# Two metaformer layers on one core: where dt's softplus is made, who copies the carried columns, and how far ahead scans are served

## The chip, the cores and the metric

The kernel runs on one core of a Trainium2 chip, as one program with one launch. The metric is the device time of an execution in microseconds. Before the change it is 5492.92 us, the median of three runs (5492.4 to 5493.44). An execution recorded by the hardware profiler took 5501.81 us; the span of its instructions is 5500.0 us. All times below come from that profiled execution unless the three runs are named.

A core has TensorE (PE in the profile), VectorE (DVE), ScalarE (ACT), GpSimd (POOL) and SyncE (SP, which only issues DMAs here). Each takes its instructions from a queue of its own, in order; semaphores tie the queues together.

## The reference

Input x is (4, 384, 32, 32) in float32. Layer 0 adds a selective scan over four directions of the image (rows and columns, forward and backward) and then a feed-forward network whose weights are Kronecker products. Layer 1 adds a Mamba block, with two halves of 384 inner channels, and then a mixture of four experts of which each token uses two. The part that the change touches is the selective scan, which both layers have:

```
dt = softplus(dts @ W_dt + bias)                  # softplus(v) = ln(1 + exp(v))
step(h, t):                                       # for each channel d and state n
    h  = exp(dt[d,t] * A[d,n]) * h + dt[d,t] * u[d,t] * B[n,t]
    y[d,t] = sum over n of h[d,n] * C[n,t]
```

There are 16 states, 384 channels in a pass, and 1024 positions in a sequence. The recurrence runs over t, so the second half of a sequence starts from the h that the first half left.

## The kernel before

**Passes and steps.** Sequences are cut into halves of T = 512 columns. A pass is one half of one direction (layer 0) or one half of one group of 384 channels (layer 1). There are 32 + 16 = 48 passes; the order of the passes mixes the layers and batches (L1362). A pass has three chunks of 128 channels and four groups of four states, so 12 steps, 576 in all. A step works on four tiles x = 0..3, each with 32 channels times 4 states on the 128 partitions and 512 columns along the free dimension. Every second pass is marked "first": it starts from zero and leaves its last column to the other half (the column at T - 1, or at 0 for a direction that runs backwards).

**A step.** ScalarE makes four decays exp(dt A) into the four PSUM tiles `da` (`decay`, L1483 to L1487). GpSimd makes s = dtu * B for all four at once, 128 x 2048 (`times_b`, L1481). VectorE runs the recurrence with one scan instruction for each x (`scan`, L1489 to L1501). The first scans of a step write into `da` in PSUM, and VectorE then multiplies them with C into s (`times_c`, L1526); the others write into s in place, and GpSimd multiplies those with C (`times_c_pool`, L1535). TensorE sums over the states into the PSUM tile `acc` (`add`, L1512 to L1517), and after four steps VectorE adds `acc` to the result (`gather`; L593, L597, L599, L819). There are four s tiles, so the product with B of step i waits for the sum of step i - 4.

**How many of a step's four products VectorE takes** is decided by `split` (L1620): if GpSimd is far ahead of the time at which its next product with B is needed (by more than SPARE), VectorE takes two; if it is less than C1 ahead, all four; else three. `share` holds the answer.

**The carried columns.** In a first pass, VectorE copies the last column of each scanned tile to the tile `state`, two copies behind each pair of scans (`keep_state`, L1503 to L1510). In the other half the scan takes its start from there.

**dt.** `prep_pass` (L464 to L501) makes dt for a whole pass: three matmuls (L476), for each of them an addition of the bias from PSUM into the SBUF tile `dt` (L485), then |v|, exp(-|v|) and ln(1 + .) over all 1536 columns in SBUF (L490), and dt = max(v, 0) + that on VectorE (L492). GpSimd multiplies with u (L497). Both tiles go to DRAM and are read back, spread over the partitions, part by part (`spread_out`, `spread_pass`; the loads of `dts` are issued on ScalarE's queue).

**The order of the instructions** is fixed when the program is built. A planner (`Plan.run`) keeps a clock for every engine and an estimated cost for each operation, and always emits what can start first. The scans and what they need are main streams: `decays` on ScalarE, `cs` and `bs` on GpSimd, `gathers` and `main` on VectorE, `adds` on TensorE. Everything else (layer norms, feed-forward network, projections, routing, experts, `prep_pass`) runs as side lanes that name, with `yield`, the engine and the cost of what comes next. `choose` (L1632) lets a side operation of ScalarE or GpSimd go ahead of a main one if it ends before that one is due. The due time comes from `needed` (L1585), which takes the next instruction of VectorE's stream and adds STEP for each step and an offset AT within the step. An `Op` has a cost and, for `adds`, a lag: the planner lets it begin that much later than its inputs' end. Three PSUM tiles `ps` serve all side work, taken and given back one at a time.

Of the kernel before, what the change touches and what calls it, by code (L numbers as in the profile page):

```python
# [12 lines left out]
AF = mybir.ActivationFunctionType  # L13
ALU = mybir.AluOpType
# [11 lines left out]
T = 512  # L26
# [224 lines left out]
def layers(ctx, tc, ins, out, const):  # L251
# [212 lines left out]
    def prep_pass(v, p, of_u):  # L464


        q, h = v["q"], v["h"]
        spread = dram.tile([2, NC, QP, NG, T], F32, tag="dts", name="dts", bufs=3)
        dt, dtu = yield from tmp.two(True)
        if v["layer"]:  # L470
            yield SP, LOAD
            nc.sync.dma_start(out=dtw[dt_rows(q), :], in_=ins["w_dt1"][:, v["c0"] * P : (v["c0"] + NC) * P])
        for c in range(NC):
            pd = yield from ps.take(True)
            yield PE, 1.2
            nc.tensor.matmul(  # L476
                pd,
                lhsT=dtw[dt_rows(q), c * P : (c + 1) * P],
                rhs=xd[dt_rows(q), cols(h)],
                start=True,  # L480
                stop=True,
            )
            bias = pv(v["dtb"], v["c0"] + c, 1)
            yield ACT, 0.7
            nc.scalar.activation(dt[:, c, :], pd, AF.Identity, bias=bias)  # L485
            ps.give(pd)

        for func, of, more in ((AF.Abs, dt, {}), (AF.Exp, dtu, {"scale": -1.0}), (AF.Ln, dtu, {"bias": 1.0})):
            yield ACT, 1.45
            nc.scalar.activation(dtu, of, func, **more)  # L490
        yield DVE, 3.15
        nc.vector.scalar_tensor_tensor(dt, dt, 0.0, dtu, ALU.max, ALU.add)  # L492
        spread_out(spread[0], dt)
        for c in range(NC):
            yield POOL, 1.3 if len(of_u(dt[:, c, :], c)) == 1 else 1.75
            for (to, u), (by, _) in zip(of_u(dtu[:, c, :], c), of_u(dt[:, c, :], c)):
                nc.gpsimd.tensor_tensor(to, by, u[:, c], ALU.mult)  # L497
        tmp.give(dt)
        yield SP, LOAD
        spread_out(spread[1], dtu)  # L500
        tmp.give(dtu)  # L501
        st["spread", p] = spread
# [986 lines left out]
    def scan(i, x):  # L1489
        p, j = steps[i]  # L1490
        v = passes[p]
        way = slice(None, None, -1) if v["rev"] else slice(None)
        s = ss[i % NSR][:, x, way]
        d = das[x][:, way]
        in_psum = x < share[i] if x else True
        nc.vector.tensor_tensor_scan(  # L1496
            d if in_psum else s, d, s, 0.0 if v["first"] else state[:, v["slot"], j, x : x + 1], ALU.mult, ALU.add
        )
        if not in_psum:
            plan.skip.add(("mult", i, x))  # L1500
            plan.end["da free", i, x] = plan.free[DVE]  # L1501

    def keep_state(i, of):  # L1503

        p, j = steps[i]
        v = passes[p]
        at = 0 if v["rev"] else T - 1
        for x in (2 * of, 2 * of + 1):
            src = das[x] if x < share[i] else ss[i % NSR][:, x, :]
            nc.vector.tensor_copy(state[:, v["slot"], j, x : x + 1], src[:, at : at + 1])  # L1510

    def add(i):  # L1512

# [21 lines left out]
    def times_c_pool(i):  # L1535
        m = share[i]
        s = ss[i % NSR]
        nc.gpsimd.tensor_tensor(s[:, m:, :], s[:, m:, :], rep(cts[i % 4], NG - m), ALU.mult)  # L1538
        for x in range(m, NG):
            plan.end["part", i, x] = plan.end["c", i]  # L1540

    STEP, C1, SPARE = 7.1, 1.29, 2.5
    C = (0.0, 3.5, 2.42, C1, 0.0)
    share = dict.fromkeys(range(N), 3)
    main, gathers, decays, bs, cs, bl, cl, adds = ([] for _ in range(8))

    AT = {"scan": (0.0, 1.27, 3.9, 5.17), "mult": (2.54, 3.22, 6.44, STEP), "state": (2.54, 6.44)}
    for i in range(N):
        p, part, m = place(i)
        v = passes[p]  # L1550
        first = v["first"]
        after = ("state", i, 1) if first else ("scan", i, NG - 1)
        ring = [("add", i - NSR)] if i >= NSR else []
        rows = ("quad", v["q"]["n"])
        if part == 0:
            of_b = [rows] + ([("b", i - 4)] if p else [])
            of_c = [rows] + ([("part", i - 4, x) for x in range(NG)] if p else [])
            bl.append(Op(("bt", p, m), LOAD, of_b, lambda p=p, m=m: load(p, m, NS, bts)))
            cl.append(Op(("ct", p, m), LOAD, of_c, lambda p=p, m=m: load(p, m, 0, cts)))
        bs.append(Op(("b", i), 4.58, [("dtu", p, part), ("bt", p, m), *ring], lambda i=i: times_b(i)))  # L1560
        for x in range(NG):
            free = [("da free", i - 1, x)] if i else []
            decays.append(Op(("da", i, x), 0.69, [("dt", p, part, x // 2), *free], lambda i=i, x=x: decay(i, x)))
        for what, x in (
            ("scan", 0), ("scan", 1), ("state", 0), ("mult", 0), ("mult", 1),
            ("scan", 2), ("scan", 3), ("state", 1), ("mult", 2), ("mult", 3),
        ):
            if what == "scan":
                op = Op((what, i, x), 1.22 if first else 1.28, [("da", i, x), ("b", i)], lambda i=i, x=x: scan(i, x))
            elif what == "state":  # L1570
                if not first:
                    continue
                op = Op((what, i, x), 0.16, [], lambda i=i, x=x: keep_state(i, x))
            else:
                op = Op((what, i, x), 0.69, [("ct", p, m)], lambda i=i, x=x: times_c(i, x))
            main.append(op)
        cs.append(Op(("c", i), C1, [("ct", p, m), after, ("split", i)], lambda i=i: times_c_pool(i)))
        wait = [("gather", (i // 4 - 1) // NC, (i // 4 - 1) % NC)] if m == 0 and i else []
        adds.append(Op(("add", i), 1.0, [("part", i, x) for x in range(NG)] + wait, lambda i=i: add(i), 1.5))
        if m == 3:  # L1580
            cost = 1.35 if v["layer"] == 0 and v["k"] % 2 else 0.75
            room = [] if v["layer"] else [("have", "y", v["b"])]
            gathers.append(Op(("gather", p, part), cost, [("add", i), *room], lambda p=p, c=part: gather(p, c)))

    def needed(plan, i, x):  # L1585

        op = plan.head(DVE, 1)
        if op is None:
            return plan.free[DVE]
        what, j, k = op.key  # L1590
        return max(plan.free[DVE], plan.now) + (i - j) * STEP + x - AT[what][k]

    def due_b(plan):

# [37 lines left out]
    def choose(plan, e, mains, side):  # L1632
        if e == POOL:
            return pool_choice(plan, mains, side)
        if e == DVE:
            for n, (t, k, op) in enumerate(mains):
                if op.key[0] == "scan" and op.key[2] == 1:
                    i = op.key[1]
                    share[i] = split(plan, i, t + 3.6)
                    plan.streams[POOL][0][i].cost = C[share[i]]  # L1640
        best = min(mains, key=lambda x: (x[0], x[1])) if mains else None
        main_of = (best[0], (best[1], best[2])) if best else None
        side_of = (side[0], side[3]) if side else None
        if side is None or main_of is None and e in (SP, PE, DVE):
            return main_of if side is None else side_of
        start, want = side[0], side[3].want
        aged = plan.now - (side[3].ready() + LAG) > age(side[3], e)
        if e == ACT:
            head = plan.head(ACT, 0)
            if head is None:  # L1650
                return side_of
            due = needed(plan, head.key[1], AT["scan"][head.key[2]]) - head.cost - LAG
            if best and best[0] <= start and not aged:
                return main_of
            if start + want[1] <= due or aged:
                return side_of
            return main_of
        if e == PE:
            d, a = plan.head(DVE, 1), plan.head(PE, 0)
            behind = (d.key[1] if d else N) - (a.key[1] if a else N)  # L1660
            if behind > 1 and best[0] <= start:
                return main_of
            return side_of if start <= best[0] + (0.3 if side[3].rank < LOW else -0.3) else main_of
        if e == DVE:
            return side_of if start <= best[0] + 0.1 else main_of
        return side_of if start <= best[0] else main_of
# [5 lines left out]


SWITCH = 2.6
LOAD = 3.0
AGE = {PE: 8.0, ACT: 6.0, POOL: 8.0, DVE: 0.0, SP: 0.0}

# [97 lines left out]
```

## Time and profile before

| | |
|---|---|
| median of three runs | 5492.92 us |
| profiled execution | 5501.81 us |
| its span | 5500.0 us |
| first scan begins, last scan ends | 92 us, 4763 us |
| L1496, the scans on VectorE (2304) | 2771.8 us, 1.21 to 1.27 us each |
| L1487, the decays on ScalarE (2304) | 1520.2 us, 684 ns each |
| L1516, the sums over states on TensorE | 1021.4 us |
| mean granted clock of TensorE | 0.802 |

The busy time of an engine is the sum over its instructions; an engine that waits isn't busy. In the rows by instruction the columns are the line, the engine, the operation, what is written and read, the shape, the count, then the busy time with the mean duration of one in ns, and last how long the engine was idle just before these instructions and what ended that idle time. TensorE's float32 matmuls show two records for each matmul of the program. The row of 40 digits has one digit for each fortieth of the span, the busy share in tenths.

### The profile page before, as it was taken

How to read it: one execution, taken by the hardware profiler on the slowest of the kernel's cores; microseconds unless marked ns; L12 is line 12 of the kernel's file. 1: busy time of each engine (PE TensorE's matmuls, PEld its weight loads, DVE VectorE, ACT ScalarE, POOL GpSimd, SP SyncE). 2: the span in 40 equal slices, each digit the busy share in tenths (PEclk: the TensorE clock that was granted, in tenths of full speed). 3: DMA queues.
4: the chain of work that ended last, by engine and by line, in shares of the span. 5: the costliest groups of instructions: out<-in, count | busy, mean ns of one | idle time of the engine just before them, and what ended most of it. 6: DMA issues, size and time to landing. Idle time of an engine off the chain costs nothing. (4 is left out here: it accounts for less than half of the span.)

```text
span 5500.0 us, 48538 instructions
## 1 busy us (share of the span) xinstructions
PE 4028.5 (73%) x13780; PEld 1779.3 (32%) x13780; DVE 4249.6 (77%) x5670; ACT 3089.9 (56%) x4683; POOL 4280.5 (78%) x1533
## 2 busy tenths in 40 slices
PE   4444467763654788787777878887888876898998
PEld 1000012210121333333334422334323322566775
DVE  4999999988888999888887889898988889510000
ACT  3444457664444577675554667775776654444342
POOL 4999999899898999898887989998988899500101
PEclk7555578775766888898887888898888877899997
DMA  3335464443343554446565554555545444456554
GB/s 112 130 136 198 161 206 157 145 133 128 129 131 122 193 162 142 162 160 195 200 218 169 179 159 140 189 169 192 177 159 177 156 155 162 153 167 198 173 172 154
DMA packets 429094, 896.32 MB, mean 163 GB/s; under 512 B 74612, under 2 KB 176152, under 8 KB 410392
## 3 DMA queue, kind: packets, MB, share of 16 engines
q1 hardware_dynamic: 371608, 701.82, 39.9%
q10 hardware_dynamic: 49024, 166.22, 8.9%
q0 software_dynamic: 8192, 25.17, 1.4%
q8 instruction: 109, 1.79, 0.1%
q14 instruction: 161, 1.32, 0.1%
HBM read 718.11 MB, written 174.95 MB: 162 GB/s over the span
## 5 line engine op out<-in xcount | busy, mean ns | idle before, releaser
L1481 POOL TENSOR_TENSOR s<-dtus,bt 128x2048 f32<-128x2048 f32 x576 | 2620.0, 4553 | 202.9 <-PE acc L1516 101.9
L1487 ACT ACTIVATE da<-dts,a 128x512 f32<-128x512 f32 x2304 | 1520.2, 684 | 1185.4 <-DVE s L1527 835.7
L1516 PE MATMUL acc<-s,four 128*32 128x512 f32 x4608 | 1021.4, 754 | 726.4 <-POOL s L1538 521.3
L1538 POOL TENSOR_TENSOR s<-s,ct 128x1024 f32<-128x1024 f32 (+1 forms) x535 | 1254.8, 2346 | 151.4 <-DVE s L1496 69.8
L1496 DVE TENSOR_TENSOR_SCAN da<-da,s 128x512 f32<-128x512 f32 x617 | 725.3, 1218 | 103.6 <-ACT da L1487 53.8
L1527 DVE TENSOR_TENSOR s<-da,ct 128x512 f32<-128x512 f32 x1242 | 796.5, 680 | 0.2
L1496 DVE TENSOR_TENSOR_SCAN da<-da,state,s 128x512 f32<-128x512 f32 x625 | 770.0, 1272 | 29.2 <-ACT da L1487 17.0
L1496 DVE TENSOR_TENSOR_SCAN s<-da,state,s 128x512 f32<-128x512 f32 x527 | 649.9, 1269 | 42.6 <-ACT da L1487 42.6
L1496 DVE TENSOR_TENSOR_SCAN s<-da,s 128x512 f32<-128x512 f32 x535 | 626.7, 1207 | 14.8 <-ACT da L1487 14.5
L1516 PEld LDWEIGHTS acc<-s,four 128*32 128x32 f32 x4608 | 145.1, 119 | 1406.5 <-POOL s L1538 754.4
L1211 PE MATMUL ps<-tmp,mw 128*128 128x256 f32 (+1 forms) x1884 | 411.7, 375 | 22.3 <-ACT tmp L1183 6.6
L1231 PE MATMUL ps<-mw,tmp 128*128 128x384 f32 x1048 | 402.0, 533 | 21.4 <-ACT tmp L1277 8.5
L1211 PEld LDWEIGHTS ps<-tmp,mw 128*128 128x128 f32 x1884 | 336.9, 203 | 143.7 <-issue 30.5
L708 PE MATMUL ps<-big,w 128*128 128x512 f32 x576 | 302.2, 671 | 83.8 <-DMA w<-in_w_in_dram 80.1
L1322 POOL DMA_INDIRECT tmp<-ys,slot x42 | 40.5, 964 | 349.5 <-DMA ys<-bt 323.2
L497 POOL TENSOR_TENSOR tmp<-tmp,big 128x256 f32<-128x256 f32 (+1 forms) x192 | 198.4, 1058 | 115.5 <-DVE tmp L492 113.6
L1231 PEld LDWEIGHTS ps<-mw,tmp 128*128 128x128 f32 x1048 | 208.8, 207 | 242.0 <-issue 86.6
L476 PE MATMUL ps<-xd,dtw 12*128 12x512 f32 (+1 forms) x288 | 205.6, 817 | 90.0 <-DMA dtw<-in_w_dt_dram 65.1
L492 DVE SCALAR_TENSOR_TENSOR tmp<-tmp,tmp 128x1536 f32<-128x1536 f32 x48 | 262.8, 5475 | 6.5 <-ACT tmp L490 6.2
L1345 DVE TENSOR_TENSOR tmp<-tmp,da 128x384 f32<-128x384 f32 x5 | 2.8, 555 | 336.1 <-PE da L1340 336.1
L490 ACT ACTIVATE tmp<-tmp 128x1536 f32<-128x1536 f32 x144 | 212.3, 1474 | 2.1 <-ACT da L1487 0.6
L708 PEld LDWEIGHTS ps<-big,w 128*128 128x128 f32 x576 | 118.0, 214 | 261.0 <-issue 197.6
(376 smaller groups left out, 5210.6 us busy)
## 6 DMA issues: line engine op xcount, KB each, us to landing
mw<-in_w_dram SPq DMA_DIRECT2D x426, 384.0 KB
dts<-dts ACTq DMA_DIRECT2D x288, 512.0 KB
dtus<-dts SPq DMA_DIRECT2D x144, 1024.0 KB
dts<-tmp SPq DMA_DIRECT2D x384, 192.0 KB
bt<-rows SPq DMA_DIRECT2D x192, 256.0 KB
ct<-rows SPq DMA_DIRECT2D x192, 256.0 KB
dts<-in_w_dram SPq DMA_DIRECT2D x102, 384.0 KB
ys<-t SPq DMA_DIRECT2D x32, 768.0 KB
```

What stands on the lines that cost most here:

```text
L476: nc.tensor.matmul(pd, lhsT=dtw[dt_rows(q), c * P : (c + 1) * P], rhs=xd[dt_rows(q), cols(h)], start=True, stop=True,)
L490: nc.scalar.activation(dtu, of, func, **more)
L492: nc.vector.scalar_tensor_tensor(dt, dt, 0.0, dtu, ALU.max, ALU.add)
L708: nc.tensor.matmul(pi, lhsT=w[:, c, :], rhs=u[:, c], start=c == 0, stop=c == NC - 1)
L1211: nc.tensor.matmul(ph[:, k * width : (k + 1) * width], lhsT=w[:, c, k * P : (k + 1) * P], rhs=turned[:, c], start=c == 0, stop=c == NC - 1,)
L1231: nc.tensor.matmul(py[k][:, :D], lhsT=by_f(hids[half_], width)[:, at_ + f, k * P : (k + 1) * P], rhs=w[:, f], start=2 * q + f == 0, stop=2 ...
L1481: nc.gpsimd.tensor_tensor(ss[i % NSR], dtus[part_of(i) % 2], rep(bts[i % 4], NG), ALU.mult)
L1487: nc.scalar.activation(das[x], dts[(2 * part_of(i) + x // 2) % 3][:, x % 2, :], AF.Exp, scale=v["a"][:, g, m : m + 1])
L1496: nc.vector.tensor_tensor_scan(d if in_psum else s, d, s, 0.0 if v["first"] else state[:, v["slot"], j, x : x + 1], ALU.mult, ALU.add)
L1516: nc.tensor.matmul(acc[x * QP : (x + 1) * QP, :], lhsT=four, rhs=ss[i % NSR][:, x, :], start=m == 0, stop=m == 3)
L1527: nc.vector.tensor_tensor(ss[i % NSR][:, x, :], das[x], cts[i % 4], ALU.mult)
L1538: nc.gpsimd.tensor_tensor(s[:, m:, :], s[:, m:, :], rep(cts[i % 4], NG - m), ALU.mult)
```

## The change

It has three parts, which share one diff.

- dt: for each third of the channels, max(v, 0) is written to SBUF, and |v|, exp(-|v|) and ln(1 + .) are made in place in the PSUM tile; VectorE adds the two, 512 columns at a time. The tile `ps` is given back behind that addition.
- Carried columns: tiles scanned in PSUM are copied by ScalarE, one column each, in the stream of the decays, ahead of the decay that overwrites the same tile. Tiles scanned in place in s are copied by GpSimd in one instruction ahead of its product with C. VectorE copies none.
- Planning: due times are EARLY = 1.5 us earlier; SPARE is 3.7 where it was 2.5; the lag of `adds` is 0.8 where it was 1.5; the costs of dt's operations and of the copies are those of the new instructions.

```diff
@@ prep_pass
             yield ACT, 0.7
-            nc.scalar.activation(dt[:, c, :], pd, AF.Identity, bias=bias)
+            nc.scalar.activation(dt[:, c, :], pd, AF.Relu, bias=bias)
+            for func, more in ((AF.Abs, {"bias": bias}), (AF.Exp, {"scale": -1.0}), (AF.Ln, {"bias": 1.0})):
+                yield ACT, 0.7
+                nc.scalar.activation(pd, pd, func, **more)
+            yield DVE, 0.7
+            nc.vector.tensor_tensor(dt[:, c, :], dt[:, c, :], pd, ALU.add)
             ps.give(pd)
-
-        for func, of, more in ((AF.Abs, dt, {}), (AF.Exp, dtu, {"scale": -1.0}), (AF.Ln, dtu, {"bias": 1.0})):
-            yield ACT, 1.45
-            nc.scalar.activation(dtu, of, func, **more)
-        yield DVE, 3.15
-        nc.vector.scalar_tensor_tensor(dt, dt, 0.0, dtu, ALU.max, ALU.add)
@@ scan
         if not in_psum:
             plan.skip.add(("mult", i, x))
+            plan.skip.add(("state", i, x))
@@ keep_state
-    def keep_state(i, of):
+    def last_column(i):
+        return 0 if passes[steps[i][0]]["rev"] else T - 1
+
+    def keep_state(i, x):
         p, j = steps[i]
-        v = passes[p]
-        at = 0 if v["rev"] else T - 1
-        for x in (2 * of, 2 * of + 1):
-            src = das[x] if x < share[i] else ss[i % NSR][:, x, :]
-            nc.vector.tensor_copy(state[:, v["slot"], j, x : x + 1], src[:, at : at + 1])
+        at = last_column(i)
+        nc.scalar.copy(state[:, passes[p]["slot"], j, x : x + 1], das[x][:, at : at + 1])
@@ times_c_pool
+        p, j = steps[i]
+        if passes[p]["first"]:
+            at = last_column(i)
+            to = state[:, passes[p]["slot"], j, m:].unsqueeze(2)
+            nc.gpsimd.tensor_copy(to, s[:, m:, at : at + 1])
         nc.gpsimd.tensor_tensor(s[:, m:, :], s[:, m:, :], rep(cts[i % 4], NG - m), ALU.mult)
@@ streams
-    STEP, C1, SPARE = 7.1, 1.29, 2.5
+    STEP, C1, SPARE = 7.1, 1.29, 3.7
-        after = ("state", i, 1) if first else ("scan", i, NG - 1)
+        after = ("scan", i, NG - 1)
         for x in range(NG):
             free = [("da free", i - 1, x)] if i else []
+            if i and passes[steps[i - 1][0]]["first"]:
+                decays.append(Op(("state", i - 1, x), 0.22, [("scan", i - 1, x)], lambda i=i, x=x: keep_state(i - 1, x)))
             decays.append(Op(("da", i, x), 0.69, [("dt", p, part, x // 2), *free], lambda i=i, x=x: decay(i, x)))
-        adds.append(Op(("add", i), 1.0, [("part", i, x) for x in range(NG)] + wait, lambda i=i: add(i), 1.5))
+        adds.append(Op(("add", i), 1.0, [("part", i, x) for x in range(NG)] + wait, lambda i=i: add(i), 0.8))
@@ needed
-        return max(plan.free[DVE], plan.now) + (i - j) * STEP + x - AT[what][k]
+        return max(plan.free[DVE], plan.now) + (i - j) * STEP + x - AT[what][k] - EARLY
@@ choose, for ScalarE
-            due = needed(plan, head.key[1], AT["scan"][head.key[2]]) - head.cost - LAG
+            step = head.key[1] + (head.key[0] == "state")
+            due = needed(plan, step, AT["scan"][head.key[2]]) - head.cost - LAG
@@ constants
+EARLY = 1.5
```

The state copies also leave VectorE's stream and the table AT, which only listed them.

More of the change, by code (lines that the diff above doesn't have):

```diff
@@ L1545, in layers @@
     main, gathers, decays, bs, cs, bl, cl, adds = ([] for _ in range(8))
-    AT = {"scan": (0.0, 1.27, 3.9, 5.17), "mult": (2.54, 3.22, 6.44, STEP), "state": (2.54, 6.44)}
+    AT = {"scan": (0.0, 1.27, 3.9, 5.17), "mult": (2.54, 3.22, 6.44, STEP)}
     for i in range(N):
@@ L1562, in layers @@
             free = [("da free", i - 1, x)] if i else []
+            if i and passes[steps[i - 1][0]]["first"]:
+                decays.append(Op(("state", i - 1, x), 0.22, [("scan", i - 1, x)], lambda i=i, x=x: keep_state(i - 1, x)))
             decays.append(Op(("da", i, x), 0.69, [("dt", p, part, x // 2), *free], lambda i=i, x=x: decay(i, x)))
         for what, x in (
-            ("scan", 0), ("scan", 1), ("state", 0), ("mult", 0), ("mult", 1),
-            ("scan", 2), ("scan", 3), ("state", 1), ("mult", 2), ("mult", 3),
+            ("scan", 0), ("scan", 1), ("mult", 0), ("mult", 1), ("scan", 2), ("scan", 3), ("mult", 2), ("mult", 3),
         ):
@@ L1569, in layers @@
                 op = Op((what, i, x), 1.22 if first else 1.28, [("da", i, x), ("b", i)], lambda i=i, x=x: scan(i, x))
[L1570 to L1573, printed above, removed]
             else:
```

## The prediction

> **What bounds the kernel now.** I read the page's busy shares first, then the busy time by stretches, then the groups of instructions, then the waits, and last one short piece of the timeline.
>
> ```profile
> PE 4028.5 (73%) x13780; PEld 1779.3 (32%) x13780; DVE 4249.6 (77%) x5670; ACT 3089.9 (56%) x4683; POOL 4280.5 (78%) x1533
> DVE  4999999988888999888887889898988889510000
> POOL 4999999899898999898887989998988899500101
> ```
>
> By stretches of the span (from and to, length, then the busy time of each engine with its instructions):
>
> ```profile
> core 0: us, PE busy (x) PEld busy (x) DVE busy (x) ACT busy (x) POOL busy (x), PEclk, DMA share, GB/s
> 92.00:4763.00 4671.00, 3304.09 (x10863) 1270.27 (x10864) 4192.77 (x5478) 2771.27 (x4160) 4214.35 (x1466) 0.78 0.50 162
> ...
> 92.00:687.50 595.50, 267.43 (x766) 45.55 (x766) 574.95 (x736) 268.22 (x383) 580.08 (x194) 0.56 0.45 151
> 1787.50:4537.50 2750.00, 2211.51 (x7597) 953.39 (x7597) 2425.46 (x3153) 1783.69 (x2718) 2448.74 (x861) 0.85 0.53 173
> 4763.00:5500.00 737.00, 680.45 (x2811) 493.72 (x2809) 30.80 (x92) 287.91 (x483) 56.43 (x55) 0.92 0.56 175
> ```
>
> VectorE and GpSimd are both nearly full until the last scan and empty after it. The first scan starts at 92 us and the last ends at 4763 us, so the loop is 4671 us for 576 steps (8.11 us each), with VectorE idle for 478 us of it and GpSimd for 457. Early on (92 to 687) both are 97% busy; once feed-forward and expert work is mixed in (1787 to 4537) both fall to 88 and 89%, and TensorE rises to 80%. The 737 us behind the loop are a tail of TensorE work, 92% busy. The end is therefore loop plus tail, and the two must be added separately.
>
> ```profile
> L1481 POOL TENSOR_TENSOR s<-dtus,bt 128x2048 f32<-128x2048 f32 x576 | 2620.0, 4553 | 202.9 <-PE acc L1516 101.9 <-issue 52.6 <-DMA dtus<-dts 42.0
> L1527 DVE TENSOR_TENSOR s<-da,ct 128x512 f32<-128x512 f32 x1242 | 796.5, 680 | 0.2
> L492 DVE SCALAR_TENSOR_TENSOR tmp<-tmp,tmp 128x1536 f32<-128x1536 f32 x48 | 262.8, 5475 | 6.5 <-ACT tmp L490 6.2
> L490 ACT ACTIVATE tmp<-tmp 128x1536 f32<-128x1536 f32 x144 | 212.3, 1474 | 2.1 <-ACT da L1487 0.6
> L1510 DVE COPY state<-da 128x1 f32<-128x1 f32 x617 | 84.9, 153 | 0.1
> L1510 DVE COPY state<-s 128x1 f32<-128x1 f32 x535 | 71.2, 142 | 0.1
> ...
> L1538 POOL TENSOR_TENSOR s<-s,ct 128x1024 f32<-128x1024 f32 x527 | 1244.6, 2363 | 149.4 <-DVE s L1496 69.8 <-DVE state L1510 57.7 <-issue 13.2
> L1538 POOL TENSOR_TENSOR s<-s,ct 128x512 f32<-128x512 f32 x8 | 10.2, 1272 | 2.0 <-DVE state L1510 1.9
> ```
>
> The reader is to see L492: 5475 ns for 1536 columns, where the 512-column operation of L1527 takes 680. The timeline tells why:
>
> ```profile
> 2518.98 5.51 DVE L492 SCALAR_TENSOR_TENSOR tmp<-tmp,tmp 128x1536 f32<-128x1536 f32 x1 [0.22 <-ACT tmp L490]
> ...
> 2518.34 4.54 POOL L1481 TENSOR_TENSOR s<-dtus,bt 128x2048 f32<-128x2048 f32 x1
> ```
>
> GpSimd's product ends at 2522.88 and L492 at 2524.49, 1.6 us later; its fastest execution took 1732 ns. So L492, with both inputs in SBUF, stands still for about 3.7 us until GpSimd's instruction is over.
>
> **VectorE, part by part.** The carried columns leave it: 1152 copies, 84.9 + 71.2 = -156 us. L492 leaves: -263 us. In its place come 144 additions of 512 columns with one operand in PSUM; L1527 and L593 are that kind (680 and 679 ns, never over 725), so +98 us. The third item isn't in the diff's words: the larger SPARE and the earlier due times make the splitter give VectorE more. In the built order the products on VectorE go from 1242 to 1467, 225 x 0.680 = +153 us. Sum: -156 - 263 + 98 + 153 = **-168 us**, so 4193 becomes 4025 in the loop.
>
> A rule is weighed here. The Trainium skill, "SBUF — State Buffer", section "SBUF: two separate sides", says that a VectorE operation with two SBUF inputs, or one in a two-port mode, takes turns with GpSimd for a whole instruction, and names an fp32 copy from SBUF to SBUF as such a mode. For L492 the row shows it. For the 535 copies out of s the rule would promise up to half a product's 4.55 us each, 2.3 x 535 = 1230 us to be won; the row says 142 ns (as from PSUM), so I take 71 us.
>
> **GpSimd.** Its products with C go from 527 of 1024 columns and 8 of 512 to 276 and 285: 1254.8 becomes 276 x 2.363 + 285 x 1.272 = 1015, so -240 us. It gains 284 copies of one or two columns. The trace has no such copy; its 128x1 memsets took about 0.10 us, its 128x128 select 0.29, so 28 to 83 us, and I take 0.2 each, +57, between the two, as a copy reads and writes. Below nothing is excluded. Sum **-183 us**: 4214 becomes 4031. Each copy waits for the fourth scan as the product behind it did before, so it adds no wait; behind it stand that product and the next product with B, which a later scan needs.
>
> **ScalarE.** Out go 97.8 us (L485) and 212.3 (L490); in come 4 x 144 activations of 512 columns at 0.68 (L422 and L429, into or out of PSUM, show 679 and 687 ns), +392, and 743 copies of one column at 0.19 (the 128x3 copies of L733 and L743: 182 and 194), +141. Together +223 us, 2771 to about 2994, some 67% of the new loop. It is hidden in the 1185 us for which ScalarE sits idle ahead of L1487. A rule speaks against the split: "Perfetto Trace Analysis", section "Optimizing Scalar/DVE Operations", prefers fewer, larger operations because each pays for its data access (about 93 ns on SBUF, 51 on PSUM, seen twice over in a profile). By it a third of an operation costs 40 ns more, 432 x 0.04 = 17 us; by the rows 679 - 491 = 188 ns more, 81 us. I take the rows. If the cover fails, scans wait for it (rival C). Each state copy waits for a scan and stands ahead of the next decay in the same buffer, which waits for a later instruction anyway. The ACT-issued loads of dts stand in this same queue, unchanged in number; SP's queue has the same 3146 instructions.
>
> **The PSUM bank.** A piece now holds one of three banks for five instructions instead of one, about 2.7 us longer, 144 x 2.7 = 390 us of 3 x 4671, under 3%. It delays only side work; what that does is in the tail's count below. VectorE's additions wait for ScalarE as L492 did (6.2 us in all); three times that is 19 us at most, none taken.
>
> **Planned times.** Every scan's inputs are due 1.5 us earlier. Scans now wait 127.9 us for L1487 and 61 for GpSimd. Ends: nothing, or all 189; I take a third, -60. Against it, the planner now believes that accumulation into acc starts 0.7 us sooner, while the eight records of one take about 1.9 us, so the gathers (L593, L597, L599, L819; 111 us of waits in 49 cases) are queued earlier: 49 x 0.7 = +34, ends 0 and 144 x 0.7 = 101.
>
> **The tail.** In the built order 1601 TensorE instructions stand behind the last accumulation instead of 1461: one expert block more (32 of L1231, 36 of L1211) and eight more combining pieces less two (42 of L1340, 21 of L1338, some others). At two records each and the rows' busy time by record (0.384, 0.219, 0.247, 0.318) this is 25 + 16 + 21 + 13 + 4 = 79 us, at 92% busy **+85 us**: 822. The same work leaves the loop.
>
> **Sum.** VectorE: 4025 + 478 - 60 + 34 = 4477. GpSimd: 4031 + 457 less its 46 us of waits for L492 = 4442, which ends earlier. Start 92 + 3 (dt's first pass in three chains), loop 4477, tail 822: span 5394, a profiled execution of 5396 against 5501.8. The median shown is 8.9 lower than that execution: **5387 us**, about 2% faster, own range 5320 to 5455.
>
> **Rivals.**
> A. The waits shrink more. VectorE no longer falls 3.7 us behind the plan 48 times, and other engines wait less for it. For: GpSimd waits 102 us on acc and 129 on VectorE. Against: the gathers. VectorE's idle at 380: loop 4405, time 5315.
> B. Slower: the later stretches are set by when TensorE's answers come. There TensorE is 80% busy in one queue, with expert runs of 5 us, and of VectorE's 325 idle us in 1787 to 4537 most are waits for its results (L593 50.9, L409 29.4, L1345 29.1). Then the freed time behind 1787 turns into such waits; only the first 1696 us shorten, by 4% of VectorE's 1572 = 63, and the tail adds 85 + 3: 5493 + 25 = 5518. It decides as soon as the loop gives back less than 88 us. Against: TensorE also loses 79 us there.
> C. ScalarE becomes late: half of its small copies' 141 us reaches the scans, 5387 + 70 = 5457.
> That the change does not do what it says is excluded for the instructions (the order shows them); its margin of 1.5 us may simply not be felt, which is +60 and within the likeliest's range.
>
> **How the numbers follow.** Likeliest 0.46, A 0.14, C 0.17, B 0.23. About 0.2%, 11 us, is what a measurement of this kernel can tell from no change. Faster: 0.45 + 0.14 + 0.14 = 0.73; same 0.05 (edges of C and B); slower 0.22. The range 5300 to 5520 leaves out the lower half of A and the upper half of B.
>
> **What would show it.** The last scan at 4570 us or so, no L492-like row over 1 us on VectorE, additions at 0.68, GpSimd's copies at 0.1 to 0.3, a tail of 820. Wrong: a last scan behind 4675, gathers' waits far over 150 us, scans' waits for L1487 over 200, copies on GpSimd of over 0.5.

## The result, and the profile after

The changed kernel takes 5507.09 us, the median of 12 runs (5495.72 to 5521.72); beside it the kernel before took 5489.9 (12 runs). The ratio is 1.0035, with a 95% interval of 1.0025 to 1.0046: slower by a third of a per cent. The forecast was 5387. The time lies inside its range, 5300 to 5520, but on the other side of the old time and outside the 5320 to 5455 of the likeliest case.

The profiled execution of the changed kernel took 5521.72 us, span 5519.9. Busy time by engine, and then by the two stretches that the forecast added up, the loop from the first scan to the last and the tail behind it (columns as before: length, then PE, PEld, DVE, ACT, POOL):

```profile
PE 4182.1 (76%) x13780; PEld 1792.7 (32%) x13780; DVE 4092.4 (74%) x4839; ACT 3215.4 (58%) x5716; POOL 4071.5 (74%) x1843
```

```profile
89.00:4718.00 4629.00, 3390.58 (x10571) 1235.13 (x10573) 4031.04 (x4637) 2878.26 (x5148) 3997.47 (x1768) 0.80 0.49 161
4718.00:5520.00 802.00, 748.15 (x3105) 542.27 (x3101) 35.24 (x100) 307.04 (x524) 64.28 (x64) 0.92 0.54 173
```

VectorE's work in the loop fell from 4193 to 4031 us and GpSimd's from 4214 to 3997. The loop fell only from 4671 to 4629. So VectorE's idle time rose from 478 to 598 us, GpSimd's from 457 to 632, and the tail grew from 737 to 802. The work went away as forecast; the time did not. The granted clock of TensorE is no reason: it was 0.814 here and 0.802 before. (An engine's busy time in these lines counts overlapping records once, so it is less than the sum over its instructions: before, VectorE's groups add up to about 4484 us and its busy time is 4249.6.)

Cut where step 480 of the 576 begins, the loop falls into two parts that behave differently. Before:

```profile
92.00:3934.00 3842.00, 2661.48 (x8740) 1007.40 (x8741) 3478.07 (x4477) 2269.23 (x3386) 3492.93 (x1202) 0.78 0.50 162
3934.00:4763.00 829.00, 642.62 (x2124) 262.87 (x2123) 714.70 (x1002) 502.04 (x775) 721.41 (x265) 0.82 0.48 160
```

After:

```profile
89.00:3858.00 3769.00, 2714.73 (x8287) 939.14 (x8287) 3335.79 (x3792) 2328.63 (x4175) 3311.48 (x1459) 0.78 0.49 161
3858.00:4718.00 860.00, 675.86 (x2284) 295.99 (x2286) 695.25 (x846) 549.62 (x974) 685.99 (x310) 0.86 0.50 164
```

The first 480 steps take 73 us less. The last 96 take 31 us more and the tail 65 more, so the end takes back more than the first part gains. In the last 96 steps TensorE has 33 us more to do, and VectorE is idle for 165 us instead of 114.

The groups of instructions that the change touches, after:

```profile
L1528 DVE TENSOR_TENSOR s<-da,ct 128x512 f32<-128x512 f32 x1467 | 948.5, 678 | 107.7 <-ACT state L1511 106.9
L1544 POOL TENSOR_TENSOR s<-s,ct 128x512 f32<-128x512 f32 x285 | 362.1, 1271 | 45.0 <-DVE s L1496 30.9 <-DMA dts<-tmp 1.1
L489 ACT ACTIVATE ps<-ps 128x512 f32<-128x512 f32 x288 | 164.4, 571 | 5.7 <-ACT state L1511 2.6
L1511 ACT COPY state<-da 128x1 f32<-128x1 f32 x743 | 115.3, 155 | 98.1 <-DVE da L1496 65.5 <-DVE s L1528 29.5 <-ACT xd L805 1.2
L491 DVE TENSOR_TENSOR tmp<-tmp,ps 128x512 f32<-128x512 f32 x144 | 97.3, 676 | 25.9 <-ACT ps L489 25.7
L1543 POOL COPY state<-s 128x2 f32<-128x2 f32 x125 | 23.6, 189 | 39.6 <-DVE s L1496 37.0 <-DMA ct<-rows 2.4
```

The first row is the news. Before, VectorE's 1242 products with C were idle for 0.2 us in all ahead of them; now they wait 106.9 us, for ScalarE's copy of a carried column. The product needs nothing that the copy makes. Both read the same PSUM tile, and the program orders the two: where the copy was put into the order first, the product waits until ScalarE's queue has come to it. (The Trainium skill, "PSUM — Partial Sum Buffer", section "PSUM bank collisions raise a hardware error", says that the compiler's scheduler adds such a dependency between instructions of two engines that touch the same bank in the same 32 partitions, two reads included; the row shows the wait, and no run here leaves the order away.)

A piece of the timeline of the changed kernel shows what that means (start, length, engine, line; in brackets the idle time before it and what ended it):

```profile
3156.63 1.17 ACT L577 COPY xd<-ps 44x512 f32<-44x512 f32 x2 [9.57 <-PE ps L571]
...
3158.18 0.69 ACT L1487 ACTIVATE da<-dts,a 128x512 f32<-128x512 f32 x1 [0.39 <-ACT xd L577]
3158.90 0.16 ACT L1511 COPY state<-da 128x1 f32<-128x1 f32 x1
3159.09 0.69 ACT L1487 ACTIVATE da<-dts,a 128x512 f32<-128x512 f32 x1
3159.72 0.15 ACT L1511 COPY state<-da 128x1 f32<-128x1 f32 x1
3159.91 0.69 DVE L1528 TENSOR_TENSOR s<-da,ct 128x512 f32<-128x512 f32 x1 [8.60 <-ACT state L1511]
```

ScalarE stood at L577, a side operation, for 9.57 us because TensorE's matmul was late. Behind it in the queue lay two copies of 0.15 us. VectorE stood still for 8.60 us until the second of them was done.

VectorE's waits inside the loop, summed by what ended them (us; the last column also has waits for DMAs and those without a known end):

| | TensorE | ScalarE's copies | decays | GpSimd | ScalarE, other | all |
|---|---|---|---|---|---|---|
| before | 266 | - | 128 | 61 | 28 | 489 |
| after | 313 | 124 | 50 | 71 | 44 | 607 |

### The profile page after: what moved, and what is told of

The parts are those of the page before. It is cut to its first block, busy times and chain, and to the rows that moved or that the text cites. A ratio compares the mean times of both kernels' runs of the same rounds, so it can differ in the third digit from the quotient of the medians.

```text
span 5519.9 us, 48747 instructions
## 1 busy us (share of the span) xinstructions
PE 4182.1 (76%) x13780; PEld 1792.7 (32%) x13780; DVE 4092.4 (74%) x4839; ACT 3215.4 (58%) x5716; POOL 4071.5 (74%) x1843
## 5 line engine op out<-in xcount | busy, mean ns | idle before, releaser
L1517 PE MATMUL acc<-s,four 128*32 128x512 f32 x4608 | 1165.4, 747 | 741.1 <-POOL s L1544 574.9
L1544 POOL TENSOR_TENSOR s<-s,ct 128x1024 f32<-128x1024 f32 (+1 forms) x561 | 1010.9, 1803 | 152.4 <-DVE s L1496 116.7
L1528 DVE TENSOR_TENSOR s<-da,ct 128x512 f32<-128x512 f32 x1467 | 948.5, 678 | 107.7 <-ACT state L1511 106.9
L1496 DVE TENSOR_TENSOR_SCAN da<-da,state,s 128x512 f32<-128x512 f32 x724 | 901.3, 1277 | 60.0 <-POOL s L1481 34.6
L1496 DVE TENSOR_TENSOR_SCAN da<-da,s 128x512 f32<-128x512 f32 x743 | 879.9, 1216 | 68.9 <-POOL s L1481 36.4
L1496 DVE TENSOR_TENSOR_SCAN s<-da,state,s 128x512 f32<-128x512 f32 x428 | 531.8, 1268 | 7.3 <-ACT da L1487 7.3
L1496 DVE TENSOR_TENSOR_SCAN s<-da,s 128x512 f32<-128x512 f32 x409 | 483.3, 1205 | 2.8 <-ACT da L1487 2.7
L1211 PE MATMUL ps<-tmp,mw 128*128 128x256 f32 (+1 forms) x1776 | 378.6, 371 | 16.5 <-ACT tmp L665 5.9
L1211 PEld LDWEIGHTS ps<-tmp,mw 128*128 128x128 f32 x1776 | 312.7, 203 | 124.9 <-issue 38.5
L418 PE MATMUL ps<-tmp,mean_w 128*128 128x512 f32 x276 | 149.7, 686 | 46.2 <-ACT tmp L414 34.2
```

The lines of the kernel that those rows point to most:

```text
L418: nc.tensor.matmul(pq, lhsT=mean_w, rhs=sq[:, c, :], start=c == 0, stop=c == NC - 1)
L1211: nc.tensor.matmul(ph[:, k * width : (k + 1) * width], lhsT=w[:, c, k * P : (k + 1) * P], rhs=turned[:, c], start=c == 0, stop=c == NC - 1,)
L1496: nc.vector.tensor_tensor_scan(d if in_psum else s, d, s, 0.0 if v["first"] else state[:, v["slot"], j, x : x + 1], ALU.mult, ALU.add)
L1517: nc.tensor.matmul(acc[x * QP : (x + 1) * QP, :], lhsT=four, rhs=ss[i % NSR][:, x, :], start=m == 0, stop=m == 3)
L1528: nc.vector.tensor_tensor(ss[i % NSR][:, x, :], das[x], cts[i % 4], ALU.mult)
```

## The experiments

Loop, tail, busy and idle times are those of each kernel's profiled execution; the ratio is to the kernel before, run on the same chip between them.

| kernel | ratio, 95% interval | loop | tail | VectorE busy, idle | GpSimd busy, idle |
|---|---|---|---|---|---|
| before | 1 | 4671 | 737 | 4193, 478 | 4214, 457 |
| dt alone | 0.9873 (0.9845 to 0.9901) | 4543 | 782 | 4045, 498 | 4142, 401 |
| copies alone | 1.0019 (1.0008 to 1.0029) | 4638 | 765 | 4057, 581 | 4213, 425 |
| planning alone | 1.0058 (1.0039 to 1.0078) | 4709 | 725 | 4206, 503 | 4031, 678 |
| dt + copies | 1.0017 (1.0007 to 1.0026) | 4621 | 799 | 3944, 677 | 4150, 471 |
| dt + planning | 0.9923 (0.9906 to 0.9939) | 4631 | 746 | 4152, 479 | 3965, 666 |
| all three (the change) | 1.0035 (1.0025 to 1.0046) | 4629 | 802 | 4031, 598 | 3997, 632 |
| dt + SPARE | 0.9790 (0.9774 to 0.9807) | 4539 | 755 | 4055, 484 | 4123, 416 |

**The parts alone and in pairs.** Each of these kernels is the one before with some hunks of the diff and without the others.

dt alone: the hunk of `prep_pass`.

> The kernel before with dt's part alone. VectorE's work falls by 263 - 98 - 40 x 0.68 = 138 us; the built order has 1555 TensorE instructions in the tail instead of 1461 (+47 us at 0.50 each). Theory 1 (nothing is wrong with this part): loop about 4671 - 130 = 4540, time about 5410. Theory 2 (waits for TensorE take its place): loop 4650 or more, time about 5520.

Measured 5423.7 us, theory 1's figure within 14 us. Nothing is wrong with this part: VectorE has 148 us less to do and the loop is 128 us shorter.

Copies alone: the hunks of `scan`, `keep_state`, `times_c_pool` and the streams, without the constants.

> The kernel before with the carried columns' part alone (ScalarE copies 664, GpSimd 245 pieces; VectorE has 57 more products, so 156 - 39 = 117 us less work; tail 1510 instructions, +25 us). Theory 1 (products wait for ScalarE's copies): a wait of VectorE for the copies of 80 to 130 us appears, loop 4650 to 4690, time 5490 to 5530. Theory 2: no such wait of size, the loop shortens but little because TensorE's answers are late, time about 5490 too, with the waits on acc and ps up by 80 or more.

Measured 5504.1 us. VectorE has 135 us less to do, 56 of them because L492 became cheaper (206.9 us where it was 262.8), and 103 us more idle time. Of its waits, 80 us are for ScalarE's copies, those for GpSimd rise from 61 to 132 and those for decays fall from 128 to 74. The waits for TensorE are not up by 80, so of the two theories this is the first, but the waits for GpSimd were in neither.

Planning alone: these constants on the kernel before.

```diff
-    STEP, C1, SPARE = 7.1, 1.29, 2.5
+    STEP, C1, SPARE = 7.1, 1.29, 3.7
-        adds.append(Op(("add", i), 1.0, ..., lambda i=i: add(i), 1.5))
+        adds.append(Op(("add", i), 1.0, ..., lambda i=i: add(i), 0.8))
-        return max(plan.free[DVE], plan.now) + (i - j) * STEP + x - AT[what][k]
+        return max(plan.free[DVE], plan.now) + (i - j) * STEP + x - AT[what][k] - EARLY
```

> The kernel before with the planning part alone (EARLY 1.5, SPARE 3.7, lag 0.8). VectorE has 198 more products (+135 us), GpSimd correspondingly less; tail 1426 instructions (-17 us). If the margin does what it did in the changed kernel (scans' waits for the decays 128 to 50 us, gathers' waits 111 to 140): VectorE's busy time +135, waits -50, loop about 4750, time about 5560. If VectorE's work does not bound the loop (theory 2): loop within 30 us of 4671, time about 5480.

Measured 5527.6 us, between the two. GpSimd has 183 us less to do and idles 221 us more. VectorE has 198 products more but only 13 us more work, because L492 became cheaper:

```profile
L492 DVE SCALAR_TENSOR_TENSOR tmp<-tmp,tmp x48: 1732/3242/6377, 67.0 to 4586.8; 128x1536 f32<-128x1536 f32 x48
```

(minimum, median and maximum in ns). Its median was 5538 ns before. That GpSimd idles more is not the whole reason: in the kernel with the copies alone GpSimd idled 425 us, less than the 457 of before, and L492's mean still fell, from 5475 to 4311 ns. Either way dt's part and the planning part win the same microseconds in part, and their gains must not be added. The scans' waits for decays and GpSimd, which the earlier due times were to shorten, are 191 us, as good as the 189 of before.

dt and copies; dt and planning:

> The changed kernel with the old planning constants (SPARE 2.5, lag 1.5, no EARLY): dt's part and the copies' part. If the parts add: 5424 + 0.0019 x 5496 = about 5434 us, tail 1589 instructions. Theory 3 (the planning constants are what spoils the change): 5400 to 5450. Theory 1 (copies ahead of products on ScalarE spoil it, more so as dt's part also fills ScalarE's queue with 288 more activations): 5480 or more with VectorE waiting 100 us or more for the copies.

> dt's part and the planning constants, the carried columns copied by VectorE as before; tail 1456 instructions. If the parts add: 5424 + 0.0058 x 5496 = 5456. Theory 3 (planning gives VectorE 225 products more, +153 us, while GpSimd idles for it): VectorE's busy time near 4045 + 125 = 4170, GpSimd's idle time 550 or more, loop about 4680, time about 5430 to 5500. Theory 1: without the copies on ScalarE the change wins: 5400 or less.

Measured 5505.1 and 5457.3 us. With the copies on top of dt, VectorE loses another 101 us of work and the loop becomes 78 us **longer**: its idle time rises by 179 us, 126 of it waiting for the copies and 64 more waiting for GpSimd. With the planning constants on top of dt, the loop is 88 us longer, and this is where it shows, GpSimd's idle time:

```profile
POOL s L1481 <- PE acc L1516: 217.4, 93, 10.1
POOL s L1538 <- DVE state L1510: 126.3, 68, 13.6
```

(waits of GpSimd in the loop: us in total, times, longest). GpSimd comes back to its ring of four s tiles before they are free (92 us with dt alone) and waits for VectorE, to which the splitter has given 184 products of GpSimd's.

**The planning constants, one by one, on dt's part.** The edits are single lines of the hunk above.

> dt's part and SPARE 3.7 alone. VectorE has 28 more products than with dt's part alone (+19 us), tail 1474 instead of 1555 (-40 us). Theory 3 with SPARE as its cause: 5440 or more. If SPARE is harmless: 5400 to 5425.

> dt's part and EARLY 1.5 alone. VectorE has 25 more products than with dt's part alone (+17 us), tail 1524 instead of 1555 (-15 us). If the margin works as meant, scans' waits for decays and for GpSimd fall from 157 us by a third or more and the time is 5380 to 5410; if GpSimd's products with C are put off by it, GpSimd's waits for acc rise from 92 us to 150 or more and the time is 5440 or more.

> dt's part with SPARE 3.7 and EARLY 1.5, lag as before. Each of the two alone moved 25 to 28 products to VectorE; together 182 (1464), as in the whole planning part. Theory 3 (the two add up to a lead of 5.2 us that GpSimd seldom has, so VectorE takes three or four products although GpSimd then idles): VectorE +124 us, GpSimd's idle 550 or more, loop about 4640, time about 5470, like dt with the whole planning part (5457). If the lag is the cause instead: 5390 to 5420.

Measured 5385.6 (ratio 0.9790), 5428.5 (0.9868, interval 0.9851 to 0.9884) and 5421.8 us (0.9856, 0.9839 to 0.9872). SPARE alone doesn't hurt. EARLY alone did neither of the two things expected: the time is that of dt alone, and the scans' waits for decays and GpSimd rose from 157 to 190 us. SPARE and EARLY together give VectorE 154 products more than SPARE alone, 83 us of work, and GpSimd 191 us more idle time; the loop is 35 us longer. The time was expected at 5470 and came out at 5422; the lag adds the rest of the way to dt with all the planning (loop 4574 to 4631). I took the splitter to be how EARLY costs, and tried it:

```diff
-        ahead = due_b(plan) - max(plan.free[POOL], start)
+        ahead = due_b(plan) + EARLY - max(plan.free[POOL], start)
```

> dt's part, SPARE 3.7 and EARLY 1.5 for the due times of inputs, but the splitter of the products works with the due time without EARLY: VectorE has 1306 products (1310 without EARLY, 1464 with EARLY in the splitter too), tail 1516 instead of 1474 (+21 us). If the splitter is what EARLY costs (5421.8 against 5385.6 us): loop back at about 4540 or less, time 5380 to 5405, and any less is the margin's own gain. If the margin itself is what costs (inputs are made so early that GpSimd's other work is late): 5420 or more with the same share of products as without.

Measured 5445.4 us (0.9916, 0.9897 to 0.9935), loop 4581, with the share of products and both engines' busy time as with SPARE alone. So that theory falls: the margin costs without the splitter too. Waits of VectorE for dt's logarithms went from 32 to 73 us there, side work put off by the margin. Which delayed side operation costs most is not settled.

**The copies.** First the order of copy and product, in the changed kernel:

```diff
-                decays.append(Op(("state", i - 1, x), 0.22, [("scan", i - 1, x)], ...))
+                decays.append(Op(("state", i - 1, x), 0.22, [("mult", i - 1, x)], ...))
```

> The changed kernel, but ScalarE's copy of a carried column is queued behind VectorE's product of the same tile instead of only behind the scan. Theory 1 (the copy and the product read one PSUM tile and are ordered one behind the other, so a product waits until ScalarE's queue reaches the copy): the 106.9 + 17.6 us that VectorE waits for the copy vanish, the loop shortens from 4629 us by about 100, the tail (1524 TensorE instructions behind the last accumulation instead of 1601) by about 39: about 5380 to 5410 us. Theory 2 (VectorE's freed time turns into waits for TensorE's answers anyway): the row vanishes, but the waits on acc and ps rise by as much, loop within 20 us of 4629, time about 5470 from the tail alone.

Measured 5496.0 us (0.9997, 0.9987 to 1.0006). VectorE's products no longer wait for a copy, but the loop is 4631 us, as long as before the edit. Its first 480 steps are 29 us shorter (3740 us for 3769), its last 96 are 31 us longer (891 for 860); but a nudge alone, below, does as much. The waits sit elsewhere: decays 92 us (50), GpSimd 98 (71), copies ahead of scans 25 (18). Only the tail is shorter. As an account of the whole, theory 1 fails here; nor did the waits for TensorE take it all, 326 us (313).

Then what the copies could be worth at all, on the best base, dt + SPARE: none made, `state` zeroed once, so that second halves start from zero.

> dt's part with SPARE 3.7 (5385.6 us: loop 4539, tail 755), and no copy of a carried column by any engine: second halves start from zero, which is left out of the computation. It shows what taking 156 us of copies off VectorE can be worth at the most. Against that base VectorE has 132 us less to do (1152 copies gone, 36 products more), the tail 58 instructions more (+29 us). If VectorE's work bounds the loop: loop about 4410, time about 5285. Theory 2 (freed time turns into waits for TensorE): loop 4500 or more, time 5380 to 5420.

Measured 5357.2 us (0.9742, 0.9726 to 0.9758). The base and this one:

```profile
91.00:4630.00 4539.00, 3354.75 (x10834) 1264.03 (x10838) 4054.66 (x5640) 2795.99 (x4436) 4122.80 (x1470) 0.79 0.51 166
```

```profile
88.00:4572.00 4484.00, 3332.28 (x10730) 1248.91 (x10731) 3966.93 (x4524) 2784.94 (x4423) 4081.58 (x1466) 0.79 0.51 167
```

VectorE's busy time falls by 88 us, not 132, GpSimd's by 41, the loop by 55 and the median by 28. In this build that is all that copies at no cost, in anyone's hands, could bring: half a per cent, no more than the shuffle measured below. The rows of single copies mislead, as the timeline of the kernel before shows:

```profile
175.47 0.27 DVE L1510 COPY state<-s 128x1 f32<-128x1 f32 x2
175.67 2.35 DVE L1496 TENSOR_TENSOR_SCAN da<-da,s 128x512 f32<-128x512 f32 x2
177.93 0.28 DVE L1510 COPY state<-da 128x1 f32<-128x1 f32 x2
178.13 1.28 DVE L1527 TENSOR_TENSOR s<-da,ct 128x512 f32<-128x512 f32 x2
179.32 2.33 DVE L1496 TENSOR_TENSOR_SCAN s<-da,s 128x512 f32<-128x512 f32 x2
```

Two copies last 0.28 us by their records, but the next instruction begins 0.20 us after the first: records overlap, and a copy holds VectorE for 0.10 us, not 0.15. By the same reading a product holds it for 0.60, not 0.68.

Then each engine's copies by themselves, on the same base. The columns of the other tiles stay with VectorE, in its stream behind each pair of scans as before the change: those of tiles in PSUM where GpSimd copies, those of tiles in s where ScalarE does.

```diff
+            elif what == "keep":
+                op = Op((what, i, x), 0.16, [], lambda i=i, x=x: keep_on_vector(i, x, ...))
```

> dt's part with SPARE 3.7; GpSimd copies the columns of tiles scanned in s (270 instructions, some 51 us), VectorE those of tiles scanned in PSUM (649, as before). VectorE has about 70 us less; tail 1510 instead of 1474 (+18 us). Theory 1 (ScalarE's copies are what costs): loop about 4539 - 65 = 4475, time about 5340. If GpSimd's copies cost as much as they save: 5385 to 5405.

> dt's part with SPARE 3.7; ScalarE copies the columns of tiles scanned in PSUM (654 instructions), ahead of VectorE's product as in the change, VectorE those scanned in s. VectorE has 100 us less of copies; tail 1535 instead of 1474 (+30 us). Theory 1: VectorE waits 100 us or more for ScalarE's copies, the loop stays at 4530 or more, time 5400 to 5450. If the copies were hidden in ScalarE's idle time: loop about 4450, time about 5325.

Measured 5433.9 (0.9878, 0.9861 to 0.9894) and 5427.8 us (0.9864, 0.9848 to 0.9881): 0.9 and 0.7% above the base, where each was to save. Against the base's nudged build below (0.9819) it is 0.6 and 0.45%, so that neither kind alone is shown to cost more than a shuffle can. GpSimd's copies take 52 us off VectorE and put 52 on GpSimd, which had no more room than VectorE: loop 4571. With ScalarE's, VectorE has 53 us less to do, and waits (L1537 is the product in that kernel):

```profile
DVE da L1496 <- POOL s L1481: 115.5, 31, 25.8
DVE s L1537 <- ACT state L1511: 86.3, 21, 13.0
```

The same with the copy queued behind the product, and last the whole copies' part on this base:

> As the kernel with SPARE 3.7 in which ScalarE copies the columns of PSUM tiles (5427.8 us, loop 4556, tail 782), but each copy is queued behind VectorE's product of the tile. Tail 1530 instructions, as there. If the order of copy and product on the PSUM tile is the price: VectorE's 86 us of products waiting for copies vanish, loop about 4470, time about 5345. If ScalarE's place in the chain is the price whatever the order: the wait moves to the scans (decays and copies over 100 us together), loop 4540 to 4570, time 5410 to 5440.

> dt's part, SPARE 3.7 and the whole copies' part (ScalarE 680, GpSimd 257 instructions), without EARLY and with the old lag; tail 1653 instructions instead of 1474 (+90 us). ScalarE's copies alone cost 42 us here and GpSimd's alone 48. If they add: about 5475. If both only use up the same waits: about 5430 plus the tail's surplus of 60, 5490.

Measured 5404.3 (0.9846, 0.9824 to 0.9869), loop 4531, and 5460.0 us (0.9937, 0.9917 to 0.9957), loop 4552, tail 822. With the order turned round, 25 us of loop come back, though the two ratios' intervals overlap; decays then cost the scans 95 us in place of 35. That loop is 8 us below the base's, the tail is 24 us longer, and the time stays above it. Together the two kinds of copies cost 1.5%, about what the two alone do (0.9 and 0.7).

**The shuffle alone.** Every edit changes the planner's order everywhere. Three controls change one planned cost by 0.01 us and nothing else in the program's text (the splitter's share moves by 8 products at most):

```diff
-            decays.append(Op(("da", i, x), 0.69, ...
+            decays.append(Op(("da", i, x), 0.70, ...
```

> Control: the kernel before with the planner's cost of a decay 0.70 instead of 0.69, which changes no instruction and only shuffles the order. Tail 1480 instructions instead of 1461. If differences between builds of some tens of us mean something: 5485 to 5510. If the shuffle alone moves a build by 20 us or more, differences of that size between the other experiments can't be put down to their edit.

> Control: dt's part with SPARE 3.7 and the same nudge; tail 1504 instead of 1474 (+15 us). Order means little: 5385 to 5410. A lottery: anywhere from 5365 to 5440.

> Control: the changed kernel with the same nudge; tail 1520 instead of 1601 (-40 us), the same products and copies. If the tail's length in the changed kernel was the build's luck and not the change: about 5470; if the loop takes back what the tail gives, as in the kernel with the copies behind the products: 5490 to 5510.

Measured: before 1.0069 (1.0052 to 1.0086), dt + SPARE 0.9819 (0.9803 to 0.9836), the changed kernel 1.0009 (0.9997 to 1.0022). So a shuffle alone moves a build by 0.3 to 0.7%. The loops stay within 14 us of where they were: VectorE's idle time in them is 476, 485 and 610 us beside 478, 484 and 598, GpSimd's 454, 413 and 633 beside 457, 416 and 632. The tail moves more: the changed kernel's falls from 802 to 768. What VectorE waits for moves as well. In the nudged builds the waits for TensorE rise from 243 us before to 339 in the changed kernel (266 to 313 without the nudge); those for decays and copies together fall from 129 to 125 (128 to 175 without), of which 81 are for copies. And the cut at step 480 moves: before the change from 3842 and 829 us to 3857 and 805, in the changed kernel from 3769 and 860 to 3740 and 903. The pattern stays, a shorter first part and a longer last one. Hence the sign of the result is within the shuffle's reach; that the change fails to bring two per cent is not.

## Why the prediction was wrong

**What held.** VectorE's work: -168 forecast, -162 measured. The total held in part because errors cancel: at 0.10 us each the copies were worth about 115 us, not 156, and at 0.60 the 225 products cost about 135, not 153. L491 took 676 ns (680 forecast), GpSimd's copies 189 ns (0.2 us), its products 1011 us (1015). The scans' waits for decays and GpSimd fell by 68 us, from 189 to 121 (-60), and the gathers' waits rose from 111 to 140 us, +29 (+34). The -60 is luck as far as the margin goes: the planning constants by themselves left the scans' waits at 191 us, and EARLY on dt's part raised them. GpSimd's work fell more than forecast, by 217 us (183), ScalarE's rose less, by 107 us (223), and of the 116 between, L486 and L489 with 356 us (392) and the copies with 115 (141) account for 62; 19 lie in the tail. The three functions took 107 ns more for each third of the columns than in L490, between the 40 of the rule weighed there, which is stated for an engine that is saturated, and the 188 of the rows. The tail grew by 65 us, by 31 in the nudged build (85).

**The step that failed** is the sum's second half, "VectorE: 4025 + 478 - 60 + 34 = 4477": the idle time of before was carried over, as 452 us with the two corrections. It came to 598, 146 more. By name, 124 us of the new idle time are a wait that the forecast put at nothing, in the sentence that each state copy "stands ahead of the next decay in the same buffer, which waits for a later instruction anyway". That looked at who waits behind the copy on ScalarE, and not at who else reads the tile: VectorE's products and scans now wait for the copies. But the name is not the whole cause. In the nudged build the idle time is 610 us with 81 for the copies, and more of it stands under TensorE instead.

**Taking that wait away did not bring the gain**, which is the second half of the answer. With the copy behind the product the loop of the changed kernel was as long as ever. On the kernel with dt and SPARE, leaving out all copies shortened the loop by 55 us, for 88 us less work on VectorE and 41 less on GpSimd. dt's part shortened it by 128, for 148 and 72 less (46 of the 72 are 40 products that the splitter gave to VectorE). Both relieve the two engines in the same proportion, and yet one yields 86% and the other 63% of VectorE's saving, though with loops that a nudge moves by up to 14 us even this difference is not certain. GpSimd's idle time fell by 56 us with dt's part and by 14 without the copies. That two full engines wait for each other in turn is my reading of this; no run isolates it. The third item, 225 products moved to VectorE, was booked as a cost on one side and a saving on the other. The saving was not used: GpSimd's idle time rose from 457 to 632 us.

**The account**, each line on top of the one above: dt -1.3%, SPARE -0.8, EARLY +0.7, the lag +0.7, the copies +1.1; in all +0.35. dt and the copies stand clear of the shuffle; the copies cost 1.5% on each of two other bases with dt's part, but 0.2% on the kernel before. The planning constants as a whole cost half a per cent both on the kernel before and on dt's part; that, and the 0.7 to 0.8% of each of the three, is about the size of a shuffle.

**The rivals.** B named 5518 us, close to what was measured, but not the way. It gave the first stretch a gain of 63 us and the rest none. By the trace the changed kernel was 15 us ahead after 216 of its 576 steps, 76 after 480, and 46 at the end; in the nudged pair it was 43, 122 and 27. So the freed time did not turn into waits right behind the first stretch, but the last 96 steps gave part of it back. The waits for TensorE rose by 47 us, and by 96 in the nudged pair. B is thus not excluded as a part of the cause. C, ScalarE late, had the place right and the size wrong: it put 70 us on the scans' waits, while those for decays fell and the products waited instead. What stays open is why VectorE's idle time comes to some 600 us with the wait for the copies and without it: with the order of copy and product turned round it came back in decays, GpSimd and TensorE, in the nudged build mostly in TensorE. Nor is it settled what makes the last 96 steps of the changed kernel long.

**The version that beats both** is dt's part with SPARE 3.7 and nothing else of the change: 5385.6 us, ratio 0.9790 (0.9774 to 0.9807), and 0.9819 in its nudged build.

## What to carry to other kernels

When an operation moves to an engine that has idle time, ask who else touches its operand: a reader of the same PSUM tile on another engine may be ordered behind it, and then inherits every wait in that engine's queue. Where two engines are full and feed each other, a saving in their work need not reach the time: here 55 us of 88 in one case and 128 of 148 in another, so do not carry the old idle time over. When the main loop gets shorter, ask where the side work goes that ran beside it: here the last steps and the tail took back about what the first steps had gained. And where a planner orders everything, nudge it by a hair to learn how much of a difference is only the shuffle, before an edit is given credit for it.

## What was not expected of the hardware

The time of VectorE's operation with two SBUF inputs beside a busy GpSimd varied with the order that was built: L492's mean was 5475 ns before, 5323 in the nudged build, 4311 with the copies alone and 3375 with the planning alone, while GpSimd idled 457, 454, 425 and 678 us of the loop. GpSimd's idle time alone doesn't set it. Activations of 512 columns in place in PSUM took 571 ns for exp and ln, and 652 with a bias from SBUF, against the 680 taken for them. The record of a one-column copy lasts 155 ns on ScalarE, 189 on GpSimd and 142 to 153 on VectorE, where it held the engine for about 100.
